# State products of linear attention in column strips of TensorE, two pairs at a time, and a step of the next rotation moved

## The chip, the cores and the metric

The program runs on one NeuronCore of a Trainium2 chip. A core has a matrix engine (TensorE, PE in the profile, with its weight loads as PEld), a vector engine (VectorE, DVE), a scalar engine (ScalarE, ACT), GpSimd (POOL) and a queue that issues most transfers (SyncE, SP). Matrix products go to PSUM, from which VectorE and ScalarE read them. The metric is the device time of one execution in microseconds (us), the median of several runs; lower is better.

## The reference, cut to what matters

Two residual layers over `x` of shape (16, 256, 64, 64), float32. Each normalises its input by groups of 8 channels first. Layer 0 is a grouped 3x3 convolution whose kernels are rotated by an angle that depends on the image; layer 1 is focused linear attention with a 5x5 depthwise convolution of the values. Of layer 1:

```python
q = (relu(xt @ Wq.T + bq) + 1e-06) / scale          # xt: (B, 4096, 256)
k = (relu(k) + 1e-06) / scale                       # k, v: halves of xt @ Wkv.T + bkv
# cubed, and brought back to the norm they had:
k = k ** 3 / norm(k ** 3) * norm(k)
# 8 heads of 32 channels each
z = 1.0 / (einsum('bic,bc->bi', q, k.sum(axis=1)) + 1e-06)
kv_state = einsum('bjc,bjd->bcd', k, v)             # one 32x32 state a head
out = einsum('bic,bcd->bid', q, kv_state) * z[..., None]
out = out + depthwise5x5(v)                         # then the output projection and the residual
```

The state of a head is a sum over all 4096 tokens of a batch: 32 key channels times 32 value channels, and, with a column of ones beside the values, the sum of the keys.

## The kernel before, in words

**Stages.** The loop runs over 16 batches `b`. The 4096 tokens of a batch are 32 rows `T` of 128 tokens; a *pair* `n` is two of them (0 to 15). For each batch there is a key phase, one `key_step(b, n, made)` for each pair; then `between`; then `attention_step(b, p, chain)` for p = 1 to 17. From p = 15 on, the attention steps hold the products of the next batch's first three key pairs (`LEAD = 3`), so the key phase of batches 1 to 15 begins at n = 3, and that of batch 0 at n = 0. About 222 us go by from one batch to the next.

**A key step** (line 715). TensorE multiplies the normalised input of two token rows by the key and value weights (`key_products`, L522, 512 columns in a PSUM bank for each row; the stationary operand is every fourth token of the image, `T % BC:CH:BC`). VectorE adds the biases (`key_bias`: L530 into the key tile `r`, L533 into a value buffer `vbuf[n % 6]`) and applies the relu (L491). ScalarE takes sums of squares (`squares`, L498) before and after GpSimd has cubed the keys (`cube`, L501); VectorE forms the ratio (`ratio`, L506 and L507), GpSimd its root (`root`, L510), and ScalarE scales the keys by it (`key_scale`, L544). That chain takes two steps: step n scales pair n - 2.

**State products** (`values`, L555). Pair `n - LATE` (`LATE = 3`) is multiplied at the end of step n. For each of the two token rows and each half `hh` of the channels (four heads), the stationary operand is 128 tokens by 128 key channels, and the moving one is 128 tokens by 33 x 4: for 32 channels and the column of ones, the four heads of the half, which stand next to each other in a value buffer `[P, 2, HD + 1, NH]`. That computes every key channel of the half with every value channel of its four heads; only the blocks on the diagonal are wanted, and `gmask` leaves them over when `kvx` is formed (L564) for the products with the queries (`attend`, L648). The sums stay in two PSUM tiles `[P, 33, 4]` from the first pair to the last.

**The next rotation.** `prepare(b + 1)` is a generator that makes the rotated kernels of the next batch for its convolution. `key_step` calls `next(made, None)` twice, after the first half's biases and at the step's end, and each call goes on to the next `yield`. It computes the angles (TensorE L196, L204, L209; ScalarE L217 to L221), the bilinear weights (VectorE L241 to L253), multiplies them out on GpSimd (`products`, L266), reduces on VectorE (`reduce`, L274; `finish`, L278 and L281), copies them to where the convolution reads them on ScalarE (`spread`, L286), and computes a shift for each channel of a half (`shifts(t)`: twelve small products on TensorE, L294, in column strips; L296 to L298 on VectorE), which the eviction of the convolution adds (L368). In batches 1 to 14, `shifts(0)` comes at the end of step 10 and `shifts(1)` at the end of step 14. In batch 0 `prepare(1)` is begun at n = 4; in batch 15 there is none.

**`between`** (line 738) has the first query products (L615), the first unit of the next batch's convolution (`convolve`, L355, tiles of 32 rows by 32 columns), the end of the key chain of the last two pairs, the second query products, the state products of pairs 13, 14 and 15, the eviction of the convolution, and the first half of the depthwise convolution as products with a band matrix in four column strips (`depthwise`, L590).

**Order.** All of it stands under a manual schedule: each engine runs its instructions in the order in which the program names them. PSUM has six banks that rotate among most products (`ps`) and two tiles of its own for the states (`psk`). Key tiles `r` come from five buffers (tag `r0`), which the queries share. The SP queue has the transfers of `key_store`, `load_blocks`, `load_rows` and others, in program order too.

Of the kernel before, what the change touches and what calls it, by code (L numbers as in the profile page):

```python
# [9 lines left out]
F32 = mybir.dt.float32  # L10
# [5 lines left out]
P = 128  # L16
# [4 lines left out]
NH, HD = 8, 32  # L21
CH = 512
NCH = N // CH
NT = N // P
# [3 lines left out]
LATE, LEAD = 3, 3  # L28
# [11 lines left out]
NV = 6  # L40
# [10 lines left out]
def conv_attention(ctx: ExitStack, tc: tile.TileContext, x, consts, kw, b1, w2, b2, b2r,  # L51
                   wkv, wq, brow, srow, wp, bp, dwb, band, out):
    nc = tc.nc
    B = x.shape[0]

    def pool(name, bufs, **kw):
        return ctx.enter_context(tc.tile_pool(name=name, bufs=bufs, **kw))
# [12 lines left out]
    psk = pool("psk", 1, space=PSUM)  # L70
# [7 lines left out]
    def bank(name):  # L78
        return ps.tile([P, CH], F32, tag="bank", name=name)
# [4 lines left out]
    state = {}  # L84
# [31 lines left out]
    gmask = ct[:, K_GM:K_GM + 4]  # L116
# [25 lines left out]
    vbuf = []  # L142
# [40 lines left out]
    def prepare(b):  # L183
# [10 lines left out]
        for k in range(2):  # L194
            for t in range(2):
                nc.tensor.matmul(ph[:, k:k + 1], lhsT=w1_t[:, t, ts(k, HID)], rhs=pooled[:, t:t + 1],  # L196
                                 start=t == 0, stop=t == 1)
        h = sp.tile([HID, 2], F32, tag="h", name=f"h_{b}")
# [8 lines left out]
        for t in range(2):  # L207
            for j in range(4):
                nc.tensor.matmul(pmod[ts(j, HD), t, :], lhsT=h[:, 1:2].to_broadcast([HID, HD]),  # L209
                                 rhs=w2_t[:, C + HD * (4 * t + j):C + HD * (4 * t + j + 1)], start=True, stop=True,  # L210
                                 tile_position=(0, HD * j))
# [25 lines left out]
        def weights(t):  # L237


            u = rotp.tile([P, 18], F32, tag="u", name=f"u_{b}_{t}")  # L240
            nc.vector.tensor_scalar(u, cgrid, cs[:, 0, t:t + 1], None, ALU.mult)  # L241
            nc.vector.scalar_tensor_tensor(u, sgrid, cs[:, 1, t:t + 1], u, ALU.mult, ALU.add)
            hat = rotp.tile([P, 3, 18], F32, tag="hat", name=f"hat_{b}_{t}")
            nc.vector.tensor_scalar(hat[:, 0, :], u, -1.0, 0.0, ALU.mult, ALU.max)
            nc.vector.tensor_scalar(hat[:, 2, :], u, 0.0, None, ALU.max)
            nc.vector.tensor_add(u, hat[:, 0, :], hat[:, 2, :])
            nc.vector.tensor_scalar(hat[:, 1, :], u, -1.0, 1.0, ALU.mult, ALU.add)
            yield
            mix = rotp.tile([P, 9, 9], F32, tag="mix", name=f"mix_{b}_{t}", bufs=2)
            hx = hat[:, :, 0:9].rearrange("p k n -> p n k")  # L250
            hy = hat[:, :, 9:18].rearrange("p k n -> p n k")
            nc.vector.tensor_scalar(hat[:, :, 9:18], hat[:, :, 9:18], a[:, t:t + 1], None, ALU.mult)
            nc.vector.tensor_mul(  # L253
                mix.rearrange("p n (y x) -> p n y x", y=3),
                hy.unsqueeze(3).to_broadcast([P, 9, 3, 3]),
                hx.unsqueeze(2).to_broadcast([P, 9, 3, 3]),
            )
            base = kw_t[:, ts(t, KB)].rearrange("p (o q) -> p o q", q=9)
            nc.gpsimd.tensor_mul(base, base, mod[:, t].unsqueeze(2).to_broadcast([P, HD, 9]))
            rots.append(rotp.tile([P, 9, HD], F32, tag="rotw", name=f"rot_{b}_{t}", bufs=2))  # L260
            mixes.append(mix)
            bases.append(base)

        def products(t, n):
            tmp = xp.tile([P, 3, HD, 9], F32, tag="x", name=f"rtmp_{b}_{t}_{n}")
            nc.gpsimd.tensor_mul(  # L266
                tmp,
                mixes[t][:, 3 * n:3 * n + 3, :].unsqueeze(2).to_broadcast([P, 3, HD, 9]),
                bases[t].unsqueeze(1).to_broadcast([P, 3, HD, 9]),
            )  # L270
            return tmp

        def reduce(t, n, tmp):
            nc.vector.tensor_reduce(rots[t][:, 3 * n:3 * n + 3], tmp, AX.X, ALU.add)  # L274

        def finish(t):
            rs = rotp.tile([P, 3, HD], F32, tag="rsum", name=f"rsum_{b}_{t}")
            nc.vector.tensor_reduce(rs, rots[t].rearrange("p (r x) o -> p x o r", x=3), AX.X, ALU.add)  # L278
            sums.append(rs)

            nc.vector.tensor_add(rots[t][:, 4], rots[t][:, 4], sel[:, 0:HD])  # L281

        def spread(t, js):
            for j in js:
                for q in (t, 2 + t):
                    nc.scalar.copy(wt[ts(q, HD), j], rots[t][ts(j, HD)])  # L286
# [15 lines left out]
        for t in range(2):  # L302
            for n in range(3):
                tmp = products(t, n)
                if t == 1 and n < 2:
                    spread(0, (2 * n,))
                yield
                reduce(t, n, tmp)
                if n == 0 and t == 0:
                    yield from weights(1)  # L310
                if n == 2:
                    finish(t)
                yield
                if t == 1 and n < 2:
                    spread(0, (2 * n + 1,))
                if t == 1 and n == 0:
                    shifts(0)
        for j in range(4):
            spread(1, (j,))
# [77 lines left out]
    for name, src, bsrc in (("kv", wkv, brow[C:3 * C]), ("q", wq, brow[0:C])):  # L397
        n = src.shape[1]
# [27 lines left out]
    for (w, br), lo in zip(wl.values(), (0, 2 * C)):  # L426
# [3 lines left out]
        n = w.shape[2]  # L430
# [4 lines left out]
    for co in range(2):  # L435
        for t in range(2):
            nc.tensor.matmul(pb[:, co:co + 1], lhsT=wp_t[:, t, ts(co, P)], rhs=dwb_t[:, t:t + 1],
                             start=t == 0, stop=t == 1)
# [48 lines left out]
    def focus(r, name):  # L487
        return {"r": r, "name": name, "s": sp.tile([P, 4, 2], F32, tag="s", name=f"s_{name}", bufs=5)}
# [11 lines left out]
    def cube(f):  # L500
        nc.gpsimd.tensor_mul(f["r"], f["r2"], f["r"])  # L501
# [7 lines left out]
    def root(f):  # L509
        nc.gpsimd.tensor_tensor(f["s"][:, 3, :], f["s"][:, 2, :], phalf, ALU.pow)  # L510
# [34 lines left out]

    def values(b, n):

        if n == 0:
            state[b]["pkv"] = [psk.tile([P, HD + 1, 4], F32, tag=f"kv{hh}", name=f"pkv{hh}_{b}") for hh in range(2)]
        pkv = state[b]["pkv"]  # L550
        r = state[b]["k"].pop(n)["r"]
        for j in range(2):
            T = 2 * n + j
            for hh in range(2):
                nc.tensor.matmul(  # L555
                    pkv[hh],
                    lhsT=r[:, j, ts(hh, P)],
                    rhs=vbuf[n % NV][:, j, :, 4 * hh:4 * hh + 4],
                    start=T == 0, stop=T == NT - 1,
                )  # L560
        if n == NT // 2 - 1:
            kvx = sp.tile([P, 2, HD + 1, 4], F32, tag="kvx", name=f"kvx_{b}", bufs=1)
            for hh in range(2):
                nc.vector.tensor_mul(kvx[:, hh], pkv[hh], gmask.unsqueeze(1).to_broadcast([P, HD + 1, 4]))  # L564
            state[b]["kvx"] = kvx

    def load_blocks(b, n):
# [42 lines left out]
    def query_products(b, m):  # L610
        xq, (w, _) = state[b]["xq"].pop(m), state[b]["q"]
        pq = bank(f"pq_{b}_{m}").rearrange("p (j n) -> p j n", j=2)
        for j in range(2):
            for t in range(2):
                nc.tensor.matmul(pq[:, j, :], lhsT=xq[:, t, ts(j, P)], rhs=w[:, t, :],  # L615
                                 start=t == 0, stop=t == 1)
        f = focus(rp.tile([P, 2, C], F32, tag="r0", name=f"rq_{b}_{m}", bufs=5), f"q_{b}_{m}")
        f["pq"] = pq
        state[b]["f"][m] = f
# [93 lines left out]
    NP = NT // 2  # L713

    def key_step(b, n, made):


        k = state[b]["k"]
        key_products(b, n, 0)
        if n >= 2:  # L720
            ratio(k[n - 2], False)
            root(k[n - 2])
        if n >= 1:
            squares(k[n - 1], 0)
            cube(k[n - 1])
        if n >= 2:
            key_scale(b, n - 2)
        key_bias(b, n, 0)
        next(made, None)
        key_products(b, n, 1)  # L730
        if n >= 1:
            squares(k[n - 1], 1)
        key_bias(b, n, 1)
        if n >= LATE:
            values(b, n - LATE)
        next(made, None)

    def between(b, more):

        k, f = state[b]["k"], state[b]["f"]  # L740
        query_products(b, 0)
        if more:
            convolve(b + 1, 0)
        ratio(k[NP - 2], False)
        root(k[NP - 2])
        squares(k[NP - 1], 0)
        cube(k[NP - 1])
        key_scale(b, NP - 2)
        query_bias(b, 0)
        blocked(b, 2)  # L750
        squares(k[NP - 1], 1)
        ratio(k[NP - 1], False)
        root(k[NP - 1])
        key_scale(b, NP - 1)
        squares(f[0], 0)
        cube(f[0])
        query_products(b, 1)
        query_bias(b, 1)
        for n in range(NP - LATE, NP):
            values(b, n)  # L760
        if more:
            for q in range(4):
                evict(b + 1, 0, q)
        squares(f[0], 1)
        squares(f[1], 0)
        if more and b + 2 < B:
            load_stats(b + 2, 0)
        if more:
            load_rows(b + 1, 1)
        for c in range(0, HD, 4):  # L770
            depthwise(b, 0, c)
        if more:
            for q in range(4):
                settle(b + 1, 0, q)
# [214 lines left out]
```

## Time and profile before

| what | value |
|---|---|
| median of 3 runs (lowest to highest) | 3655.24 us (3654.7 to 3658.32) |
| the profiled execution: its time, its span | 3655.57 us, 3653.8 us |
| mean granted TensorE clock | 0.996 |
| key products L522 on PE | 964.6 us busy, 2048 records |
| state products L555, weight loads on PEld | 262.6 us busy, 2048 records, 190 ns each |
| depthwise L590 on PE | 232.5 us busy, 8192 records of 107 x 128, 273 ns each |
| shifts L294 on PE | 20.5 us busy, 768 records, 175 ns each |
| small strips L209 on PE | 5.4 us busy, 256 records of 64 x 32, 201 ns each |
| L564 on VectorE (kvx) | 32 instructions, 0.295 us each |

Times are in us unless marked ns. A row of instructions gives line, engine, operation, the program's names of what is written and read, the shape, how many there are, the time in which at least one of them ran, the mean length of one, and the idle time of the engine just before them with what ended it. One record's length (278 ns for L555) is longer than the distance of two starts, since products follow each other in a pipeline; the prediction goes by starts. In a timeline a row begins with start and length, and neighbours of one kind are merged into one row.

The key phase of batch 6, which the prediction reads, runs from about 1479 us (step 3) to 1542 us (step 15), and its `between` to 1567 us.

### The profile page before, as it was taken

Reading aid. Unit: us, or ns where it says so; the run is one execution under the profiler, and the core shown is the slowest. Engines: PE = TensorE matmul, PEld = TensorE weight load, DVE = VectorE, ACT = ScalarE, POOL = GpSimd, SP = SyncE. Lnnn points to the kernel's source line nnn. Section 1 sums busy time; section 2 is a strip of 40 time slices with the busy share of each in tenths; the row PEclk is TensorE's granted clock in tenths of the full one; section 3 lists DMA queues with packets and bytes.
Section 4 is the critical chain, followed back from the end, with each engine's and each line's share of the span. In section 5 each row is a group of like instructions: output and inputs, shape, how many; then the busy total and the mean of one; then the engine's idle time right before and its main releaser. Section 6 shows DMA issues by size and latency. Waiting matters only on the chain. (4 is left out here: it accounts for less than half of the span.)

```text
span 3653.8 us, 101966 instructions
## 1 busy us (share of the span) xinstructions
PE 3541.7 (97%) x40424; PEld 2760.6 (76%) x40424; DVE 2453.4 (67%) x6403; ACT 2019.9 (55%) x6501; POOL 1647.6 (45%) x1775
## 2 busy tenths in 40 slices
PE   5899999999999999999999999999999999999999
PEld 3577777777777778787777877777777787777878
DVE  4666668667685667767667676676856667566656
ACT  2464645556455565654646556464555655546565
POOL 3343545435354454534445444353534535344445
PEclk9999999999999999999999999999999999999999
DMA  6353553635446254452634526355362544525342
GB/s 180 110 163 100 158 168 103 189 97 160 149 128 189 79 175 139 149 174 82 181 123 152 169 97 190 100 164 155 113 189 90 163 147 141 178 82 159 95 141 103
DMA packets 219807, 513.78 MB, mean 141 GB/s; under 512 B 26645, under 2 KB 99863, under 8 KB 207044
## 3 DMA queue, kind: packets, MB, share of 16 engines
q1 hardware_dynamic: 219332, 507.26, 45.0%
q8 instruction: 320, 5.24, 0.6%
q14 instruction: 155, 1.27, 0.1%
HBM read 371.63 MB, written 135.53 MB: 139 GB/s over the span
## 5 line engine op out<-in xcount | busy, mean ns | idle before, releaser
L522 PE MATMUL pk<-wkv,x 128*128 128x512 f32 x2048 | 964.6, 612 | 0.0
L659 POOL TENSOR_TENSOR o<-o,fm 128x256 f32<-128x256 f32 x512 | 362.4, 729 | 1000.4 <-DVE o L657 861.3
L522 PEld LDWEIGHTS pk<-wkv,x 128*128 128x128 f32 x2048 | 611.5, 311 | 184.9 <-issue 2.9
L355 PE MATMUL pc<-xr,wt 32*32 32x504 f32 (+1 forms) x17856 | 618.5, 596 | 9.0 <-DMA xr<-in_x 5.6
L355 PEld LDWEIGHTS pc<-xr,wt 32*32 32x32 f32 x17856 | 359.8, 103 | 233.4 <-issue 101.3
L498 ACT ACTIVATE r_k<-rk 128x256 f32<-128x256 f32 x1024 | 416.6, 408 | 183.7 <-DVE rk L491 110.1
L677 PE MATMUL py<-oT,wp 128*128 128x256 f32 x2048 | 505.7, 390 | 0.8 <-ACT oT L669 0.7
L615 PE MATMUL pq<-wq,xq 128*128 128x256 f32 x2048 | 492.0, 383 | 5.4
L498 ACT ACTIVATE r_q<-rq 128x256 f32<-128x256 f32 x1024 | 413.7, 408 | 59.9 <-POOL rq L501 32.5
L368 ACT ACTIVATE x<-pc,shift 128x512 f32<-128x512 f32 x256 | 165.3, 690 | 487.9 <-PE pc L355 487.9
L615 PEld LDWEIGHTS pq<-wq,xq 128*128 128x128 f32 x2048 | 370.0, 191 | 67.3 <-issue 11.6
L677 PEld LDWEIGHTS py<-oT,wp 128*128 128x128 f32 x2048 | 369.2, 189 | 51.4 <-issue 3.6
L510 POOL TENSOR_TENSOR s_k<-s_k,phalf 128x2 f32<-128x2 f32 x256 | 176.5, 690 | 479.9 <-DVE s_k L507 474.8
L669 ACT COPY oT<-po 128x512 f32<-128x512 f32 x256 | 149.8, 585 | 408.1 <-PE po L667 407.6
L544 ACT ACTIVATE rk<-rk,s_k 128x256 f32<-128x256 f32 x512 | 231.7, 499 | 235.3 <-POOL s_k L510 235.2
L623 DVE TENSOR_TENSOR rq<-pq,bq 128x512 f32<-128x512 f32 x256 | 175.9, 687 | 265.8 <-PE pq L615 259.4
L501 POOL TENSOR_TENSOR rk<-r_k,rk 128x512 f32<-128x512 f32 x256 | 335.7, 1311 | 41.3 <-ACT r_k L498 39.1
L501 POOL TENSOR_TENSOR rq<-r_q,rq 128x512 f32<-128x512 f32 x256 | 330.8, 1292 | 29.9 <-issue 29.9
L555 PEld LDWEIGHTS pkv<-v,rk 128*128 128x128 f32 x2048 | 262.6, 190 | 101.7 <-issue 42.1
L530 DVE TENSOR_TENSOR rk<-pk,bkv 128x256 f32<-128x256 f32 x512 | 214.4, 419 | 183.7 <-PE pk L522 181.2
L510 POOL TENSOR_TENSOR s_q<-s_q,phalf 128x2 f32<-128x2 f32 x256 | 179.1, 700 | 325.7 <-DVE s_q L507 324.3
L555 PE MATMUL pkv<-v,rk 128*128 128x132 f32 x2048 | 270.5, 278 | 14.8 <-ACT rk L544 14.8
(128 smaller groups left out, 5389.2 us busy)
## 6 DMA issues: line engine op xcount, KB each, us to landing
vh<-vpad SPq DMA_DIRECT2D x256, 384.0 KB
vh<-vpad SPq DMA_DIRECT2D x256, 360.0 KB
vpad<-v SPq DMA_DIRECT2D x512, 128.0 KB
out<-x SPq DMA_DIRECT2D x128, 512.0 KB
xr<-in_x SPq DMA_DIRECT2D x186, 320.0 KB
xs<-in_x SPq DMA_DIRECT2D x224, 256.0 KB
xr<-in_x SPq DMA_DIRECT2D x62, 288.0 KB
xs<-in_x SPq DMA_DIRECT2D x16, 512.0 KB
```

Of the source, the lines that this page charges most:

```text
L355: nc.tensor.matmul(pcs[q].rearrange("p (r w) -> p r w", w=W)[ts(j, HD), :, to:to + n], lhsT=wt[ts(q, HD), j, k, :], rhs=g[ts(q, HD), j, r: ...
L498: nc.scalar.activation(f["r2"][:, j, :], f["r"][:, j, :], AF.Square, accum_out=f["s"][:, k, j:j + 1])
L501: nc.gpsimd.tensor_mul(f["r"], f["r2"], f["r"])
L510: nc.gpsimd.tensor_tensor(f["s"][:, 3, :], f["s"][:, 2, :], phalf, ALU.pow)
L522: nc.tensor.matmul(pm, lhsT=state[b]["x"][n // 2][:, t, T % BC:CH:BC], rhs=w[:, t, :], start=t == 0, stop=t == 1)
L530: nc.vector.tensor_add(f["r"][:, j, :], pm[:, 0:C], br[:, 0:C])
L544: nc.scalar.mul(f["r"][:, j, :], f["r"][:, j, :], f["s"][:, 3, j:j + 1])
L555: nc.tensor.matmul(pkv[hh], lhsT=r[:, j, ts(hh, P)], rhs=vbuf[n % NV][:, j, :, 4 * hh:4 * hh + 4], start=T == 0, stop=T == NT - 1,)
L615: nc.tensor.matmul(pq[:, j, :], lhsT=xq[:, t, ts(j, P)], rhs=w[:, t, :], start=t == 0, stop=t == 1)
L623: nc.vector.tensor_add(f["r"], f["pq"], state[b]["q"][1].unsqueeze(1).to_broadcast([P, 2, C]))
L659: nc.gpsimd.tensor_add(o, o, fm[:, 2 * (m % NCH) + j, :])
L677: nc.tensor.matmul(py[:, co].rearrange("p y (J c) -> p J y c", c=BC), lhsT=wp_t[:, t, ts(co, P)], rhs=oT[:, t, :].rearrange("p (J y c) -> ...
```

## The change

State products. Each half's one product of 128 key channels by 33 x 4 columns becomes four, one for each head: the stationary operand is 128 tokens by the 32 key channels of a head, the moving one 128 tokens by the 33 value columns of that head alone (every eighth float of the value buffer), and the output goes to the 32 partitions of that head, in a column strip of TensorE at `tile_position=(0, 32 * h)`. The PSUM tiles become `[P, 33]`, and only wanted blocks are computed; `kvx` is formed by the mask from the tile repeated four times, at the same size as before.

Order of the state products. Step 3 has pair 0; then every odd step n has pairs n - 4 and n - 3 (step 5 pairs 1 and 2, up to step 15 with pairs 11 and 12), and even steps have none. In `between`, pairs 13 and 14 come ahead of the second query products and pair 15 behind them.

Shift. `shifts(0)` is called two `yield`s later, in batches 1 to 14 at the end of step 11 in place of step 10, and in batch 0 in the middle of step 14 in place of step 13.

```diff
@@ prepare
-                if t == 1 and n == 0:
+                if t == 1 and n == 1:
                     shifts(0)
@@ values
-            state[b]["pkv"] = [psk.tile([P, HD + 1, 4], F32, tag=f"kv{hh}", name=f"pkv{hh}_{b}") for hh in range(2)]
+            state[b]["pkv"] = [psk.tile([P, HD + 1], F32, tag=f"kv{hh}", name=f"pkv{hh}_{b}") for hh in range(2)]
...
             for hh in range(2):
-                nc.tensor.matmul(
-                    pkv[hh],
-                    lhsT=r[:, j, ts(hh, P)],
-                    rhs=vbuf[n % NV][:, j, :, 4 * hh:4 * hh + 4],
-                    start=T == 0, stop=T == NT - 1,
-                )
+                for h in range(4):
+                    nc.tensor.matmul(
+                        pkv[hh][ts(h, HD)],
+                        lhsT=r[:, j, ts(4 * hh + h, HD)],
+                        rhs=vbuf[n % NV][:, j, :, 4 * hh + h],
+                        start=T == 0, stop=T == NT - 1,
+                        tile_position=(0, HD * h),
+                    )
...
-                nc.vector.tensor_mul(kvx[:, hh], pkv[hh], gmask.unsqueeze(1).to_broadcast([P, HD + 1, 4]))
+                nc.vector.tensor_mul(kvx[:, hh], pkv[hh].unsqueeze(2).to_broadcast([P, HD + 1, 4]),
+                                     gmask.unsqueeze(1).to_broadcast([P, HD + 1, 4]))
@@ key_step
-        if n >= LATE:
+        if n == LATE:
+            values(b, 0)
+        elif n > LATE and n % 2:
+            values(b, n - LATE - 1)
             values(b, n - LATE)
@@ between
+        for n in range(NP - LATE, NP - 1):
+            values(b, n)
         query_products(b, 1)
         query_bias(b, 1)
-        for n in range(NP - LATE, NP):
-            values(b, n)
+        values(b, NP - 1)
```

## The prediction

> **What bounds the kernel now.** I read the page first, then TensorE's timeline through one key phase and the stretch behind it, then the same stretch on VectorE, ScalarE and GpSimd.
>
> ```profile
> PE 3541.7 (97%) x40424; PEld 2760.6 (76%) x40424; DVE 2453.4 (67%) x6403; ACT 2019.9 (55%) x6501; POOL 1647.6 (45%) x1775
> L522 PEld LDWEIGHTS pk<-wkv,x 128*128 128x128 f32 x2048 | 611.5, 311 | 184.9 <-issue 2.9
> L615 PEld LDWEIGHTS pq<-wq,xq 128*128 128x128 f32 x2048 | 370.0, 191 | 67.3 <-issue 11.6
> L555 PE MATMUL pkv<-v,rk 128*128 128x132 f32 x2048 | 270.5, 278 | 14.8 <-ACT rk L544 14.8
> ```
>
> TensorE is busy 97% of the span, so any time taken off it looks like a gain. The state products (L555) are 2048 records for 1024 products in the program: an f32 product is two records. A pair n is 8 of them. But the share is a mean, and the key phase of a batch with a following rotation (batches 1 to 14) reads differently:
>
> ```profile
> 1504.10:1537.70 33.60, 32.74 (x140) 24.21 (x140) 32.88 (x64) 22.78 (x76) 25.17 (x22) 1.00 0.62 185
> ```
>
> The columns are length, then busy time of PE, weight loads, DVE, ACT, POOL. In steps 7 to 14 of batch 6 VectorE is busy 32.88 of 33.60 us, more than TensorE, which already waits (1526.91 and 1532.11, pkv for ScalarE's rk L544, 0.38 and 0.48 us by the timeline). Where does that chain leave TensorE? VectorE and GpSimd at step 5:
>
> ```profile
> 1492.86 0.42 DVE L241 TENSOR_SCALAR u<-consts,cs 128x18 f32<-128x18 f32 x1
> 1493.31 0.61 DVE L242 SCALAR_TENSOR_TENSOR u<-consts,cs,u 128x18 f32<-128x18 f32 x1
> 1491.97 1.27 POOL L501 TENSOR_TENSOR rk<-r_k,rk 128x512 f32<-128x512 f32 x1
> 1493.20 0.68 POOL L259 TENSOR_TENSOR kw<-kw,mod 128x288 f32<-128x288 f32 x1
> ```
>
> L241 takes 0.23 us at 1502.64, with GpSimd idle; here it ends as GpSimd's cube ends, and L242 as L259 ends. So VectorE is held to GpSimd here, and the cube's start goes back over the root (1491.32), ScalarE's squares behind two table loads (1486.70, 1488.36) and key_scale (1485.78) to the key products of step 3, ahead of the first state product. From there to the first query products (1543.03, which wait for ScalarE's xq) nothing on the longest chain is TensorE's.
>
> **The cost of a pair now, and of a group in strips.**
>
> ```profile
> 1512.27 1.06 PE L555 MATMUL pkv<-v,rk 128*128 128x132 f32 x8
> 1513.17 3.71 PE L522 MATMUL pk<-wkv,x 128*128 128x512 f32 x8
> 1516.72 1.06 PE L555 MATMUL pkv<-v,rk 128*128 128x132 f32 x8
> 1517.71 0.62 PE L294 MATMUL pbias<-gm,rsum 128*32 128x1 f32 x24
> 1518.26 3.82 PE L522 MATMUL pk<-wkv,x 128*128 128x512 f32 x8
> 1521.92 1.06 PE L555 MATMUL pkv<-v,rk 128*128 128x132 f32 x8
> 1486.83 0.33 PE L209 MATMUL pa<-w,h 64*32 64x32 f32 x16
> 1487.09 2.11 PE L522 MATMUL pk<-wkv,x 128*128 128x512 f32 x4
> ```
>
> Now: 1512.27 to 1513.17 is 0.90 us for a pair (0.1125 a record), and the eight key products behind it take 3.55 where eight starts 0.429 apart make 3.43: 0.12 more. So 1.02 us a pair between key products.
>
> L294 and L209 are the rows for column strips (32 columns). Going in: 1516.72 to 1517.71 is 0.99, 0.09 over the pair. Coming out: L209's last record starts 0.123 before the next key product, 0.09 over its own 0.03; then the key products take 3.66 (1518.26 to 1521.92), 0.23 over 3.43, since their weights load in the open. A group in strips between key products thus pays 0.09 + 0.09 + 0.23 = 0.41.
>
> Inside, each pair becomes 2 tokens x 2 halves x 4 heads x 2 passes = 32 records of 33 columns, 8 rounds over the four strips. Strips do overlap: L590's 256 records of 128 columns start over 7.13 us (1559.50 to 1566.63), 0.111 a round of four where one record alone streams 0.107. L209's 16 records (32 columns) are the nearest in size: after the first round they come 0.032 a round.
>
> Unknown is what the new moving operand costs: one float in eight (32 bytes apart) where the old one had four neighbours at each place. From below, L209's 0.032 (no penalty). From above, 0.116: the old record visited the same 33 places in 0.1125, so one strip's read need not be slower. The nearest row for a strided read by TensorE is the key products' weights, one float in four: the page has 311 ns beside 191 for the contiguous query weights, and where they load in the open they cost 0.23 against 0.10 (1554.88 to 1556.71 is 1.83, less eight of 0.216), a factor of 2.1 or so. 33 columns at 0.1125/132 are 0.028, times 2.1 0.058, plus the 0.005 of L590's and L209's rounds: I take 0.0635.
>
> The Trainium skill speaks against this change twice. "SBUF — State Buffer" (Door 1: The DMA port swizzle, the note on cachelines) says that SBUF has 16-byte lines and an access to a new line each time pays; the key weights agree with it (311 against 191 ns), no run here shows it for a moving operand. "TensorEngine Tiling (Array Packing)" (Instruction Overhead) says a small matmul costs some 60 cycles whatever its width; at 2.4 GHz that makes an estimate of 32 x 25 ns = 0.8 us a pair, and with it the stretch behind the key phase below would gain 0.2 us a batch, the whole some 4 us (near 3651). L209's records start 6 to 7 ns apart, which disagrees, so the sum goes by the row.
>
> So at 0.0635: one pair (step 3) 0.41 + 0.51 = 0.92 against 1.02; two pairs (steps 5, 7 ... 15) 0.41 + 1.02 = 1.43 against 2.04. A key phase saves TensorE 0.10 + 6 x 0.61 = 3.8 us.
>
> **What of it counts.** In batches 1 to 14: nothing of the 3.8. TensorE already had 1.7 us of waits between step 12 and 1543.03 and gets some 5.4; the chain above hides it. If that cover were gone, 3.8 x 14 = 53 us more; from VectorE's idle ahead of pk(5,0) (0.95 at 1492.19) at most 0.95 x 14 = 13 could come through, and I take 0, because L241 is held by the cube until 1493.24 anyway. Groups now wait for the key_scale of their second pair; behind them stand the next step's key products, but VectorE reads those later still (it does step 11's second half at 1527.09, when TensorE has ended step 12's).
>
> The shift of the first half (L294, 24 records, and VectorE's L296 to L298, 0.45 us together, no DMA) goes from step 10 to step 11, past a reduce (1.04) and a step's biases on VectorE, no SP or POOL instruction of its own. Behind values(7), values(8) it needs no way in of its own: 0.41 less 0.12 or so of TensorE's time in the covered stretch, so nothing (4 us in all without cover). Who reads the shift is the eviction at 1554.62, 25 us later. The v and rk buffers of every second pair come free a step later and are needed after the group in TensorE's order: nothing. kvx (L564) multiplies the same 132 elements: nothing.
>
> **Behind the key phase** TensorE is the bound:
>
> ```profile
> 1544.95 9.99 PE L355 MATMUL pc<-xr,wt 32*32 32x512 f32 x288
> 1554.88 1.99 PE L615 MATMUL pq<-wq,xq 128*128 128x256 f32 x8
> 1556.71 2.86 PE L555 MATMUL pkv<-v,rk 128*128 128x132 f32 x24
> 1559.50 7.20 PE L590 MATMUL pd<-vh,band 107*32 107x128 f32 x256
> ```
>
> Now, beside the query products: out of the convolution's tiles 0.09, query weights 0.10, 24 records 2.70, into strips 0.09: 2.99. After: convolution to strips 0.09, sixteen rounds 1.02, out 0.09, query weights 0.10, in 0.09, eight rounds 0.51, and none to L590, which has the same strips: 1.91. Saved 1.09. Nothing holds it back: the last two key_scales end at 1549.1 and 1552.9, well before 1554.9; the second query's bias and squares come about 1.2 us later, and ScalarE's pd copies (0.58 each against 0.87 of TensorE's) catch up inside the 7.2 us. 14 x 1.09 = 15.2.
>
> Batch 15 has no rotation and its key phase is TensorE's (55.00 of 55.00 us busy from 3490 to 3545). The last key products end earlier by 0.10 + 5 x 0.61 and the last but one pair that now stands behind them, 1.02: 4.2. There the last pair waits for its key_scale, 6.96 behind pk(15) (3540.95 to 3547.91); TensorE's work before it is then 6.1, so it still waits, and takes 0.51 where 1.10 stood: 0.6. Together 4.8. Batch 0 (VectorE and GpSimd bound too, from step 7): 1.09 and some 0.2. Sum 15.2 + 4.8 + 1.3 = 21.3. The profiled execution took 3655.57 (span 3653.8 and 1.8 around it), 0.3 over the median: 3634.
>
> **Rivals.**
> - The strided read is free (0.032 a round): 0.38 + 24 x 0.032 = 1.15 behind the key phase, 1.85 saved x 15, batch 15 near 8: 3620. For: the old records read 32-byte steps at full rate, four floats each. Against: 311 beside 191 ns.
> - The key phase's 3.8 us come through as the 97% suggests: 14 x 4.9 + 8 = 76: 3580. Against: 32.88 of 33.60.
> - The read is bound by places (0.116 a round), so the change doesn't do what it says: behind the key phase 0.38 + 2.78 = 3.17, 0.17 lost x 15, key groups 0.3 and 0.2 longer, mostly covered: 3659 to 3663.
> - Slower: strided reads of the four strips don't overlap, 4 x 0.058 = 0.234 a round. Then 6.0 against 2.99 behind the key phase, and 0.41 + 16 x 0.234 = 4.15 against 2.04 a group, 14 us a key phase less some 2 of waits: 15 us x 15 and more, 3890. It decides from about 0.115 a round on; 0.15 would give 3718. For: no row has four strided streams. Against: L590 and L209 overlap fully.
> - Longer waits lower the clock: 3.52 and 4.31 us of waiting did in batch 0 (0.66 and 0.50 granted), 0.48 didn't; the longest now is near 2.3. The cost that isn't covered is 0.6 a batch: 8 us, inside the first case's range.
>
> **How the numbers follow.** Likeliest 58%: 3634, its own range 3621 (VectorE's 0.95 comes through) to 3645 (0.075 a round, or the clock). Free read 15%, key phase through 5%, place-bound 10%, slower 12%. Range 3608 to 3660 leaves out the second rival, the slow one and a part of the third. Within 0.2% (7 us, about what a measurement tells from none) is most of the third: 0.08; slower 0.13; faster 0.79.
>
> **What would show it.** L555 as 8192 records of 33 columns; a round near 0.064 (two pairs 1.0 us and no more); 3.45 + 1.4 us steps in batch 15; in batches 1 to 14 the time from the step 3 key products to the first query as before (60 us) with TensorE's waits at pkv grown to some 5 us, and the convolution's end to L590 shortened from 4.6 to 3.5 us. A round over 0.115, or a key phase that shortens, proves me wrong.

## The result: no change, and the profile after

The changed kernel takes 3657.18 us (median of 14 runs, 3646.13 to 3662.22) beside 3656.43 (14 runs, 3651.87 to 3661.23) for the kernel before on the same chip: a ratio of 0.9998, 95% interval 0.999 to 1.0005. The profiled execution took 3649.7 us, with a span of 3647.9. The forecast was 3634, and 3657 lies outside its own range and in the part of the wide range that was given to other cases.

The first page of the changed kernel's profile:

```profile
span 3647.9 us, 114284 instructions
PE 3492.2 (96%) x46568; PEld 2653.1 (73%) x46568; DVE 2466.1 (68%) x6403; ACT 2016.4 (55%) x6501; POOL 1648.0 (45%) x1775
q8 instruction: 368, 6.03, 0.7%
```

TensorE is busy 49.5 us less and the span is only 5.9 shorter, so waits have come in its place. The third line is a DMA queue: packets, megabytes, share. It carries instructions for TensorE, 368 packets of 16,384 bytes where there were 320. TensorE's 40424 and 46568 records with a weight load each make 80848 and 93136 instructions, and with the 1149 and 1179 that its queue runs beside them (semaphores, above all) 81997 and 94315, which is 320.3 and 368.4 times 256. So one packet is 256 instructions, or about 128 records.

The groups of TensorE by form (busy us, mean ns of one, idle time just before them, and what ended it), the first line from the kernel before:

```profile
L590 PE MATMUL pd<-vh,band 107*32 107x128 f32 x8192 | 232.5, 273 | 1.1 <-issue 1.0
L594 PE MATMUL pd<-vh,band 107*32 107x128 f32 x8192 | 240.9, 275 | 18.0 <-issue 18.0
L557 PE MATMUL pkv<-v,rk 128*32 128x33 f32 x8192 | 165.9, 241 | 33.2 <-ACT rk L544 33.2
```

The state products now wait for ScalarE's keys, as foretold. The depthwise products (L590 before, L594 now) were not touched by the change, and had 1.1 us of idle time in the whole span before; now they have 18.0, ended by "issue", that is, by nothing the profile has an event for.

So I cut each batch at five records of TensorE and compared the two profiles (after minus before, us; "a batch" is the mean):

| stage of a batch | batches 1 to 14, sum | a batch | forecast a batch |
|---|---|---|---|
| key phase: first state product to first query product | -6.0 | -0.43 | 0 |
| convolution unit | -1.1 | -0.08 | 0 |
| end of the convolution to the first depthwise record | -14.8 | -1.07 (4.62 to 3.55) | -1.09 |
| depthwise, first half | **+23.4** | **+1.67** | 0 |
| from there to the next batch's first state product | -0.3 | -0.02 | 0 |

Batch 15 gives -4.2 (forecast -4.8), and the time ahead of the first state product differs by -1.6. Batch 0 gives -1.4 (forecast -1.3), but not by the forecast's terms: -1.1 behind the convolution, +0.5 in the key phase, +1.15 in the depthwise part and -2.0 in the rest. All together -5.9. The gains that were forecast are there, and the depthwise part gives them back: +24.5 us over all batches, +1.15 of it in batch 0 and none in batch 15.

TensorE's timeline behind the convolution of batch 4 shows it at its worst (start, length, merged records; in brackets the idle time):

```profile
1103.19 1.44 PE L557 MATMUL pkv<-v,rk 128*32 128x33 f32 x64
1104.56 1.99 PE L619 MATMUL pq<-wq,xq 128*128 128x256 f32 x8
1106.48 0.69 PE L557 MATMUL pkv<-v,rk 128*32 128x33 f32 x32
1106.98 2.59 PE L594 MATMUL pd<-vh,band 107*32 107x128 f32 x82
1112.24 1.08 PE L594 MATMUL pd<-vh,band 107*32 107x128 f32 x16 [2.67 <-issue]
```

After 82 of 256 depthwise records TensorE stops for 2.67 us, and the profile shows nothing that it waits for. The first half's 256 records took 7.13 us before in nearly every batch; now they take 7.1 to 11.9. The place of the break is the telling part. Counted in depthwise records from 0, the first break of a batch stands at 91 (batch 0), 89, 86, then 81, 79 (batches 4, 5), 74, 71, 69, 66, 64, 61, 59 (batches 7 to 13); where there is another it is 128 records on, and batches 3, 6 and 14 have only that one (212, 204, 184). It moves back by some 2.5 records a batch, modulo 128, which is the length of an instruction packet and no length of the program. More exactly: counted in TensorE's instructions from the program's first, every break of the depthwise products over 0.25 us (from start to start), in this profile and in those of all the other runs here, 169 in twelve executions, stands 192 or 193 past a multiple of 256.

What the DMA engines do in 1103 to 1113 us (40 slices, busy tenths; then queues):

```profile
DMA  0002929799999999999999999998410000000000
q1 hardware_dynamic: 576, 1.31, 63.1%
q8 instruction: 1, 0.02, 0.9%
...
xr<-in_x SPq DMA_DIRECT2D x4, 320.0 KB
```

Right behind the convolution come the four transfers of `load_rows(b + 1, 1)`, which fill all 16 DMA engines for nearly 6 us. TensorE's one instruction packet of this stretch starts only between 1109.2 and 1109.8, when they are nearly through, and TensorE goes on at 1112.24. Over the 21 breaks of this trace (two of them in the second half of the depthwise products) TensorE always goes on 1.23 to 1.61 us after such a packet has ended. From the block boundary one block ahead of the break to the start of the transfer it is 2.7 us in the median, the transfer takes 1.3, and from its end to the next instruction it is 1.4: 5.4 us. The 128 records of a block last 3.5 to 5.2 us in this stretch.

### The profile page after: what moved, and what is told of

Read it like the earlier page. It is cut to its first block, busy times and chain, and to the rows that moved or that the text cites. A ratio compares the mean times of both kernels' runs of the same rounds, so it can differ in the third digit from the quotient of the medians.

```text
span 3647.9 us, 114284 instructions
## 1 busy us (share of the span) xinstructions
PE 3492.2 (96%) x46568; PEld 2653.1 (73%) x46568; DVE 2466.1 (68%) x6403; ACT 2016.4 (55%) x6501; POOL 1648.0 (45%) x1775
## 5 line engine op out<-in xcount | busy, mean ns | idle before, releaser
L522 PE MATMUL pk<-wkv,x 128*128 128x512 f32 x2048 | 981.7, 626 | 0.0
L491 DVE SCALAR_TENSOR_TENSOR rk<-rk,eps 128x512 f32<-128x512 f32 x256 | 284.7, 1112 | 8.8
L378 DVE TENSOR_TENSOR x<-x,shift 128x16 f32<-128x16 f32 x256 | 68.9, 270 | 310.7 <-ACT x L368 310.7
```

The lines of the kernel that those rows point to most:

```text
L491: nc.vector.scalar_tensor_tensor(f["r"], f["r"], 0.0, eps_t.unsqueeze(1).to_broadcast([P, 2, C]), ALU.max, ALU.add)
L522: nc.tensor.matmul(pm, lhsT=state[b]["x"][n // 2][:, t, T % BC:CH:BC], rhs=w[:, t, :], start=t == 0, stop=t == 1)
```

## The experiments

Theory F (instructions): the denser stream behind the convolution, 104 records in 3.55 us where 32 stood in 4.62, uses up a block of instructions before the next is there, since its transfer is held up by the row transfers. Theory B (places): the breaks belong to something of the depthwise products themselves, such as their operands or banks, now that strips run straight into strips. Theory C (cover): the key phase's gain of 3.8 us a batch is real, but hidden behind VectorE and GpSimd. The labels of the lines differ by the lines an edit adds. Breaks are given from the start of one record to that of the next, which is some 0.27 us more than the idle time in the rows.

**The changed kernel again**, unedited, on the same chip as the next three.

> The changed kernel once more, on one chip with the next three. Both theories: 3646 to 3662 us, as its runs so far. Theory F (TensorE runs out of instructions in the depthwise strips behind the new state products: they come in blocks of 256, and the stretch behind the convolution now holds 104 records in 3.6 us where it held 32 in 4.6): the depthwise part takes 7.7 to 12 us in batches 0 to 14 and 7.1 in batch 15, with one break of 0.3 to 3 us in each, at a place that moves back by two or three records from batch to batch and ends 1.2 to 1.5 us after an instruction transfer. Theory B (the depthwise products wait for a PSUM bank or for value blocks that now come relatively later): the breaks stand at a multiple of 32 records, the same one in every batch.

Measured: 3662.56 us (3655.78 to 3667.84) beside 3655.03, ratio 1.0018 (1.0009 to 1.0027). The key phase -5.3, the stretch to the depthwise part -15.1 and the depthwise part +23.7 over batches 1 to 14 are those of the first profile, and the breaks come at the same records. What differs is the rest of the batch, +7.8 where the first had -0.3; 5.9 of the 7.8 lie in the second half of the depthwise products, whose breaks stand at the same places of the count. The same places in two executions speak against chance and against B with a fixed record.

**Row transfers later.** The four transfers are issued in the first attention step, not in `between`; nothing is computed otherwise.

```diff
@@ between
-        if more:
-            load_rows(b + 1, 1)
@@ attention_step
             load_blocks(b, 2 * p + 14)
+            if p == 1 and more:
+                load_rows(b + 1, 1)
             load_blocks(b, 2 * p + 15)
```

> The changed kernel with the row transfers for the next convolution unit (4 of 320 KB, issued at the convolution's end) moved behind the first transfer of the first attention step, which itself waits for the depthwise part. Theory F1 (the instruction transfers are late because they queue with these rows): the breaks in the depthwise part shrink from some 1.5 us a batch to under 0.4, the depthwise part takes 7.1 to 7.5 us, and the time falls by 15 to 22 us, to 3632 to 3642. Theory F2 (the transfers are fast enough alone, only the instructions are too dense): breaks stay at 1 us or more, time 3650 to 3660. Theory B: no change of the breaks.

Measured: 3637.51 us (3634.25 to 3638.24), ratio 0.9953 (0.9941 to 0.9966), and 25 us under the changed kernel on the same chip. The depthwise part takes 7.12 to 7.14 us in every batch, and its group has 3.5 us of idle time in place of 18.0, all of it in the second half, which stands in an attention step. Batch 6, TensorE's timeline, and the DMA engines in 1103.5 to 1113.5 us (batch 4):

```profile
1551.74 0.71 PE L557 MATMUL pkv<-v,rk 128*32 128x33 f32 x32
1552.24 7.20 PE L594 MATMUL pd<-vh,band 107*32 107x128 f32 x256
1559.37 0.66 PE L635 MATMUL pt<-consts,rq 128*128 128x128 f32 x4
```
```profile
DMA  0000000200000000000000003000000000000000
q8 instruction: 2, 0.03, 1.6%
```

The 256 records run through without a break, at the same block boundaries. With the rows out of the way, the packet of the first block boundary behind the convolution starts 0.9 us after that boundary in the median (1.5 at most), where it started 3.0 after it in the changed kernel (2.3 to 5.3 in the batches that break there). That is theory F with its second half: the stream is too dense for a delayed block, not for an undelayed one.

**The boundaries moved by 64 records.** 32 small products (64 records) are put ahead of everything, once.

```diff
+    pz = bank("pad")[:, 0:1]
+    for _ in range(32):
+        nc.tensor.matmul(pz, lhsT=ident, rhs=ident[:, 0:1], start=True, stop=True)
     load_kernels(0)
```

> The changed kernel with 32 small products (64 records, 128 instructions, half a block) ahead of the first batch, so that every block boundary falls 64 records earlier. Theory F: the breaks in the depthwise part stand 64 records earlier or one block (128 records) later than before: near 27 or 155 in batch 0, 22 or 150 in batch 2; their lengths differ, the time within 3635 to 3665. Theory B: the breaks stay at the records at which they stood (91, 89, 86 in batches 0, 1, 2).

Measured: 3723.94 us (3712.84 to 3732.5), ratio 1.0191 (1.0173 to 1.0208). The breaks stand at 155, 153, 150, 148, 145 and so on to 120. Batch 12:

```profile
2952.26 3.70 PE L597 MATMUL pd<-vh,band 107*32 107x128 f32 x126
2958.89 6.64 PE L597 MATMUL pd<-vh,band 107*32 107x128 f32 x130 [2.93 <-issue]
```

The break stands at 125 of the count from 0, where the unpadded kernel has it at 61: 64 on. It goes with the count of instructions since the program's start, whatever the depthwise part is doing, and theory B falls. The size was not foreseen: each break in batches 0 to 14 now is 2.2 to 3.3 us from start to start, the depthwise part +62.4 us in all beside the kernel before, and another +22.5 lies in the rest of the batch, where the convolution units now have 16 breaks at the same places of the count. So 64 records that compute nothing cost 61 us against the unpadded kernel on the same chip. Some 11 of them are their own: they take 13.8 us at the start, and the first state product comes 11.1 us later. The other 50 come from where they put the boundaries.

**Dummies in the kernel before.** 72 one-column strip records go behind the state products of each batch; they take 0.78 us.

```diff
             values(b, n)
+        pz = bank(f"pz_{b}")[:, 0:1]
+        for k in range(36):
+            h = k % 4
+            nc.tensor.matmul(pz[ts(h, HD)], lhsT=ident[:, 0:HD], rhs=ident[:, 0:1], start=True, stop=True,
+                             tile_position=(0, HD * h))
```

> The kernel before, with 36 products of one column in column strips (72 records) between its state products and the depthwise part: as many more records there as the change brings, nothing else of it. Work of their own some 0.55 us a batch. Theory F: breaks in the depthwise part appear in most of the batches, some 1 us each; the time rises by 9 of work and 10 to 20 of breaks, to 3672 to 3685. Theory B: no breaks, 3663 to 3666.

Measured: 3707.83 us (3705.34 to 3713.25), ratio 1.0149 (1.0134 to 1.0165); the dummies themselves +12.5, the depthwise part +35.4, the rest of the batch +10. Batch 6:

```profile
1576.06 2.86 PE L555 MATMUL pkv<-v,rk 128*128 128x132 f32 x24
1578.85 0.78 PE L764 MATMUL pz<-consts 128*32 128x1 f32 x72
1579.61 2.82 PE L590 MATMUL pd<-vh,band 107*32 107x128 f32 x92
1584.76 6.45 PE L590 MATMUL pd<-vh,band 107*32 107x128 f32 x164 [2.33 <-issue]
```

With the old state products, not one of them in a strip, there are breaks now too (0.4 to 2.8 us in 15 of 16 batches), just from more instructions in hardly more time. The direction is F's, the size again was put too low.

**Row transfers later in the kernel before**, the same edit as above.

> The kernel before, with the same row transfers moved as in e2. If e2's gain were the move's alone, this one would fall by some 20 us too, to 3635 to 3640. If the row transfers only hurt where the instructions are dense (theory F1), it loses at most the 1.3 us that its own two breaks cost: 3650 to 3656.

Measured: 3654.67 us (3650.18 to 3658.77) beside 3657.99, ratio 0.9986 (0.9977 to 0.9995). The depthwise part gains 1.2 us, its two old breaks. By the ratios, 0.9953 over 0.9986, some 12 us of the 17 that the changed kernel wins with the edit belong to the change (the two were measured on different chips, each beside the kernel before).

**Without the cover.** GpSimd's nine products of the bilinear sum are cut to one, and VectorE's reduce with them; first in the kernel before, then in the changed one with the later rows.

```diff
             nc.gpsimd.tensor_mul(
-                tmp,
-                mixes[t][:, 3 * n:3 * n + 3, :].unsqueeze(2).to_broadcast([P, 3, HD, 9]),
-                bases[t].unsqueeze(1).to_broadcast([P, 3, HD, 9]),
+                tmp[:, :, :, 0:1],
+                mixes[t][:, 3 * n:3 * n + 3, 0:1].unsqueeze(2).to_broadcast([P, 3, HD, 1]),
+                bases[t][:, :, 0:1].unsqueeze(1).to_broadcast([P, 3, HD, 1]),
             )
...
-            nc.vector.tensor_reduce(rots[t][:, 3 * n:3 * n + 3], tmp, AX.X, ALU.add)
+            nc.vector.tensor_reduce(rots[t][:, 3 * n:3 * n + 3], tmp[:, :, :, 0:1], AX.X, ALU.add)
```

> The kernel before, with the bilinear sum of the rotated kernels cut from nine terms to one (GpSimd's products and VectorE's reductions have a ninth of their elements); what is computed is not the rotation. It takes the load off VectorE and GpSimd in the key phase of batches 0 to 14. Both theories: some 2 us a batch less (TensorE's waits there), 3625 to 3650. It is the base for e7.

> e2 with the same cut. Theory C (in the key phase the 3.8 us that TensorE saves are hidden by VectorE and GpSimd): now they come through in every batch as they do in batch 15, and from the first state product to the first query product it takes 3 to 4 us less than in e6 (in e2 against the kernel before: 0.4), so some 45 to 75 us under e6 in all. Rival (they are lost for another reason, the waits for the second pair's key_scale or the lowered clock): less than 1.5 us a batch, under 40 us in all.

Measured: 3619.95 us (3617.12 to 3623.59) for the old state products and 3546.82 (3544.17 to 3551.36) for the new ones, 73 apart; the first is 5 us below what was expected. The key phase of batches 1 to 14 is 55.5 us shorter with the new ones, 3.96 a batch; the later rows alone change it by 0.01 a batch in the kernel before. Windows inside one key phase of each (length, busy PE, weight loads, VectorE, ScalarE, GpSimd, clock, DMA share, GB/s): the old thin one, the new thin one, and the changed kernel itself in steps 7 to 14 of batch 6:

```profile
1487.00:1526.00 39.00, 39.00 (x187) 29.59 (x187) 25.37 (x77) 31.37 (x106) 20.99 (x26) 1.00 0.74 243
```
```profile
1452.00:1488.00 36.00, 36.00 (x372) 25.50 (x372) 29.07 (x86) 29.77 (x106) 21.22 (x27) 1.00 0.79 249
```
```profile
1503.00:1536.50 33.50, 29.99 (x296) 20.85 (x296) 32.27 (x62) 23.88 (x80) 24.58 (x22) 1.00 0.64 191
```

In the thin kernels TensorE is busy without a gap, and all it is spared becomes time. In the changed kernel VectorE is busy 32.27 of 33.50 us and TensorE 29.99: it waits, and what it was spared is gone. Theory C holds.

**Pairs one at a time.** The kernel with later rows, with the strips but the old order: one pair a step, and pairs 13 to 15 behind the second query's products.

```diff
-        if n == LATE:
-            values(b, 0)
-        elif n > LATE and n % 2:
-            values(b, n - LATE - 1)
+        if n >= LATE:
             values(b, n - LATE)
@@ between
-        for n in range(NP - LATE, NP - 1):
-            values(b, n)
         query_products(b, 1)
         query_bias(b, 1)
-        values(b, NP - 1)
+        for n in range(NP - LATE, NP):
+            values(b, n)
```

> e2 with the old order of the state products: one pair in each key step from step 3, and pairs 13, 14 and 15 behind the second query products. By the sum of the prediction: behind the key phase one way out and in less (0.1 us a batch less), in the key phase 6 x 0.41 more of TensorE's time, hidden in batches 1 to 14, some 2.5 us more in batch 15. So within 5 us of e2 if the order of the pairs brings nothing where VectorE is the bound. If working in twos matters (waits, clock), 10 us or more over e2.

Measured: 3644.79 us (3643.89 to 3654.69), ratio 0.9963 (0.995 to 0.9976) beside 0.9953 (0.9941 to 0.9966) in twos: the two can't be told apart by these. Against the profile in twos, the key phase takes 0.15 us more a batch, batch 15 2.8 in all; small breaks of 0.3 to 0.9 us are back in the depthwise part (+7.3), which was not expected. The row transfers are gone from that stretch and the packets start 0.7 us after their boundary in the median, so what is left as the reason is the density: three pairs in strips run straight into the depthwise strips, with no query products between. The order in twos is worth what the switches into and out of strips cost where TensorE is the bound, and these small breaks.

**The shift alone**, in the kernel before.

```diff
-                if t == 1 and n == 0:
+                if t == 1 and n == 1:
                     shifts(0)
```

> The kernel before with the shift's move alone (shifts(0) a step later). All theories: TensorE and VectorE do the same work in the covered stretch, within 0.1% of the kernel before; the time from the first state product to the first query product within 0.1 us a batch.

Measured: 3660.24 us beside 3659.13, ratio 1.0007 (0.9995 to 1.0018): no difference in the time. The key phase is 0.12 us shorter a batch, a little more than the 0.1 expected, and four breaks of 0.4 to 0.8 us (+2.3) stand in the depthwise part.

**Two of the four row transfers later** (`load_rows` takes the list of them; the first two stay where they were).

```diff
-        for q in range(4):
+        for q in qs:
...
-            load_rows(b + 1, 1)
+            load_rows(b + 1, 1, (0, 1))
...
             load_blocks(b, 2 * p + 14)
+            if p == 1 and more:
+                load_rows(b + 1, 1, (2, 3))
```

> The changed kernel with two of the four row transfers moved as in e2 and two left where they were. Theory F1: TensorE's next block of instructions waits for the row packets ahead of it, so half the rows mean about half the delay, and a delay under the block's own length doesn't show: breaks in the depthwise part under 0.5 us a batch or none, 3637 to 3648. If any row transfer at that place were enough: breaks as in e1, 3650 to 3662.

Measured: 3648.16 us (3642.24 to 3654.4), ratio 0.9974 (0.9965 to 0.9983). Half of the data leave 70% of the depthwise part's loss (+17.5 of +24.5), with breaks of 0.9 to 2.1 us in batches 0 to 2 and 4 to 12, and the time lies just past the one expected range and short of the other. Batch 6:

```profile
1554.21 2.38 PE L594 MATMUL pd<-vh,band 107*32 107x128 f32 x77
1557.87 5.46 PE L594 MATMUL pd<-vh,band 107*32 107x128 f32 x179 [1.28 <-issue]
```

The expected breaks under 0.5 us are missed. The packet of the first block boundary starts 3.4 us after that boundary in the median here, 3.0 with all four transfers and 0.9 with none: its delay isn't proportional to the data that stand ahead. What it queues behind, packet by packet, was not followed and stays open; so does a part of the rest of the batch, whose difference is -0.3 and +7.8 us in two executions of one kernel.

## Why the prediction was wrong, by its own steps

**The step that failed** is "Nothing holds it back: ... ScalarE's pd copies (0.58 each against 0.87 of TensorE's) catch up inside the 7.2 us". I asked of the depthwise part only whether its operands and its banks come in time, found that they do, and took over its 7.13 us. Its instructions were late. 3 x 32 strip records replace 24, so from the convolution's end to the first depthwise record 104 records go by in 3.55 us (29 a us) where 32 went by in 4.62 (7 a us), and 256 in 7.1 us follow at 36 a us. A block of 128 lasts 3.5 us at that pace, and at the breaks its successor took 5.4 in the median. The price was 24.5 us: with it the sum gives +3 in place of -21.3, and the medians differ by +0.8. The count of instructions was in the text (32 records for 8), but used for TensorE's time alone. None of the rivals had it: the one on the slower side (strips that don't overlap) was another mechanism, and refuted. That the supply is the cause is shown from four sides: taking the row transfers away ends the breaks in this order of the products, moving the count moves them by exactly as much, adding empty instructions to the old kernel makes them, and all of them stand at one place of the 256 instructions of a packet.

**The strided read**, 0.0635 a round (bounds 0.032 and 0.116): measured 0.062 to 0.063, and two pairs take 1.13 us from their start to that of the next products. (The estimate of 0.8 us a pair from the Trainium skill's "TensorEngine Tiling (Array Packing)", Instruction Overhead, is too high: eight rounds make 0.50.) The estimate from the key weights, 311 ns beside 191, met the size; that the stride is the reason is argued, since no run changes the stride alone. **Switches**: 0.09 in, 0.09 out, 0.23 of open weight loads foretold; measured 0.093 in and 0.227 of open loads, and out some 0.11, by which the next key product starts later than the last record's own 0.062. The two-step period where TensorE is the bound, sixteen starts of key products 0.429 apart and 1.43 for a group, should be 8.30; the thin changed kernel has 1463.44 - 1455.12 = 8.32:

```profile
1455.12 7.26 PE L522 MATMUL pk<-wkv,x 128*128 128x512 f32 x16
1462.30 1.21 PE L557 MATMUL pkv<-v,rk 128*32 128x33 f32 x64
1463.44 7.26 PE L522 MATMUL pk<-wkv,x 128*128 128x512 f32 x16
```

**Behind the key phase**: 1.09 a batch foretold, 1.07 measured. **The key phase** in batches 1 to 14, counted as nothing of 3.8: measured 0.43 a batch, inside the 0.95 that was put as the most, and 3.96 with the cover off. The line that proves it wrong, "a key phase that shortens", was too strict by that. **Batch 15**: 4.8 foretold, 4.2 measured; its last pair still waits for its keys, as foretold, with 0.86 us:

```profile
3539.55 1.99 PE L619 MATMUL pq<-wq,xq 128*128 128x256 f32 x8
3542.41 0.84 PE L557 MATMUL pkv<-v,rk 128*32 128x33 f32 x32 [0.86 <-ACT rk L544]
```

**The shift**: nothing, and nothing measured. **The clock rival** came true as a mechanism, and in the key phase without its price. In 13 of the 14 batches a wait of 1.97 to 2.01 us for the keys, some 40 us into the key phase, is followed by a granted clock of 0.50 for 3.4 or 6.8 us, which sets in 0.2 to 2.3 us behind the wait. A window in batch 4 (columns as above):

```profile
1071.40:1074.60 3.20, 3.20 (x5) 1.23 (x5) 3.17 (x7) 2.94 (x10) 1.97 (x3) 0.50 0.61 194
```

Five records fill the 3.20 us on TensorE, and VectorE is busy for 3.17 of them. The slower products take the place of waits: TensorE's idle time in the key phase, 0.97 us a batch before, is 4.4 in batch 6, where the clock doesn't fall, 2.9 in most of the others and 2.0 in batches 7 and 8, which have the drops of 6.8 us. (The prediction had waits of some 5.) So in time it costs nothing that can be seen: batch 6, without a drop, and batch 7, with one of 6.8 us, take 59.91 and 59.94 us from the first state product to the first query product. Not so behind the depthwise breaks of batches 4 and 10 (2.94 and 2.04 us from start to start), the two with a drop after them: their depthwise parts take 11.9 and 11.0 us, more than the 7.13 and the break together.

With the row transfers moved, the terms of the old sum come back in the stages: -15.9 behind the key phases of batches 0 to 14 and -4.2 in batch 15, with -5.1 in the key phase beyond them. The profiled span is 21.4 shorter than before, 21.3 foretold, but that these agree is luck: -5.2 in the convolution units and the depthwise part, which the move brings to the kernel before too (-5.3), and +9 elsewhere stand in the first number. The medians give 17 us, 5 of them (0.9986) the move's own; so without the breaks the change brings some 12 of the 21.3, and where the rest stays is open.

## What to carry to other kernels

Cutting a product into column strips cuts its time and multiplies its instructions: price a change by records per microsecond as well, stage by stage, and where a block of 128 records lasts less than the some 5 us that its successor took here, look at what the DMA engines do in that stretch. An idle time that ends with "issue", in a part that no edit touched, and that moves by a fixed number of records from batch to batch modulo 128, was the instruction supply here; move the bulk transfers out of the dense stretch, not the products. And compare two kernels stage by stage before believing a total of no change: here it was -15.9 behind the convolution and -14.5 elsewhere against +24.5.

## What the runs showed of the hardware

The granularity of TensorE's instruction supply: packets of 16,384 bytes, 256 instructions, and at the breaks of the changed kernel some 5.4 us in the median from a block boundary to the first instruction of the next block. The Trainium skill, "Runtime: NRT & Kernel Launch" (Instruction fetch mechanics), says that instructions are refilled in 16 KiB blocks of 256 by a DMA queue of the engine's own while the current block runs, and that crossing a boundary is "mostly hidden". The size agrees with the trace. In the first half of the depthwise products the hiding nearly holds in the kernel before (breaks of 0.71 and 0.30 us in two batches) and not here: 0.3 to 2.9 us a break in batches 0 to 14, and 2.2 to 3.3 with the boundaries moved by 64 records.

The count itself is a parameter of the time: 64 small records ahead of everything moved the median from 3662.6 to 3723.9 us, only some 11 us of it by their own time.

Waits of about 2 us were enough, in 13 of 14 batches, for the granted clock to fall to 0.50 for 3.4 or 6.8 us; in batch 6 one of 1.98 us was not, and in batch 10 one of 1.97 was.
